# Packing edges by node pairs with PSUM operands, and a fill between the row gathers, in a graph layer kernel

## The chip, the core and the metric

The kernel runs on one core of a Trainium2 chip. The metric is the device time of one execution in microseconds, lower is better. A core has five engines with their own instruction queues: TensorE (PE; its weight loads are listed as PEld), VectorE (DVE), ScalarE (ACT), GpSimd (POOL) and SyncE (SP). SBUF is the working memory of 128 partitions, PSUM the memory that TensorE writes its products to. Transfers run on the core's 16 DMA engines.

## What is computed

A graph layer over 6250 nodes with 256 features and 206,250 edges (`src`, `dst`, sorted by `dst`). The layer norm of `x` goes to two branches, whose sum is added to `x`, and a mixture of experts follows. The part that matters here is the graph branch:

```python
x = h @ W                       # 6250 x 64
el, er = x @ Wl.T, x @ Wr.T     # 6250 x 4 heads
e = jnp.exp(jax.nn.leaky_relu(el[src] + er[dst], negative_slope=0.2))
rowsum = jax.ops.segment_sum(e, src, num_segments=N)
w = e / jnp.maximum(rowsum, EPS)[src]
heads = [jax.ops.segment_sum(w[:, hd:hd + 1] * x[dst], src, num_segments=N) for hd in range(H)]
out = jax.nn.elu(jnp.stack(heads, axis=1) + b).reshape(N, 256)
```

The other branch is linear attention with 4 heads and a row norm. The experts are 8 two-layer networks with weights of 256 x 256; each node's two best are combined.

## The kernel before, in words

The nodes are 49 tiles of 128. The edges are put in a grid of 128 partitions x 1612 columns and have to be brought into the order of their source tile. The kernel has three stages.

**Preparation.** For each group of four tiles `project` (L247) loads rows, computes statistics, transposes, and multiplies with one wide weight matrix; it leaves queries, keys and values in SBUF, and 64 features and 4 right-hand scores of each node in the table `table` in device memory (68 numbers a row). Between the groups, three calls of `sort_batch` (L306) each treat 32 columns of edges, 51 batches in all. A batch compares each edge's tile number with 0 to 49 (`ob`, L320), counts with TensorE (L326), forms ranks (L330 to L365), and moves each edge's two half words (`va`, `vb`) to the partition that its rank names with a one-hot matrix (`ohp`, L372) and a product (L377). The result is `grid`: for each tile, batch and partition at most one edge. `context` (L387) computes the attention's inner matrix among the last batches. A placement stage (L472 to L515) then computes for every tile and batch where its edges go.

**Main stage.** Its order is written out by hand at L907 to L936 for 49 tiles. For each tile, `pack` (L782) moves the tile's edges to 35 columns of 128 edges with one-hot products (`ohc` L785, `rc` L791, `ohp` L799, product L804). It gives `dst_x`, the row numbers of `table`, and `loc`, the source node's place within the tile. `gather` (L824) issues 35 indirect transfers from POOL (L830), one per column. Each brings 128 rows. Rows go to buffers of seven columns, of which there are 12. `sources` (L840) makes the one-hot matrix `oh` (L842), transposes it, and picks the left-hand scores. `weights` (L860) adds the two scores and takes the exponential. `sums` (L873) multiplies each gathered row with its four weights (`v`, L879: 7 columns x 256 products) and sums over the edges of each node with TensorE (L887: a 128 x 128 one-hot matrix against 260 columns, 35 times a tile). `pack` and `gather` for a tile are issued two tiles ahead.

**Fill work.** `attention` (L518) and `finish_steps` (L603: `front`, `route`, eight times `expert`) are generators. `some_more` (L894) takes one step of them after each fifth of a tile, so that they run among the edge work, in groups of four tiles. What is left runs after the last tile (L937).

The instructions of each engine are issued in a fixed order that a scheduler at build time makes of this program. POOL's queue in the main stage holds nothing but the gathers.

Of the kernel before, what the change touches and what calls it, by code (L numbers as in the profile page):

```python
# [17 lines left out]
P = 128  # L18
GT = 4
BW = 32  # L20
PB = 16
CPT = 35
CW = 36
EB = 7
# [3 lines left out]
def tile_gps_layer(  # L28
# [40 lines left out]
    NBT = -(-EC // BW)  # L69
    NB = NT + NT % 2  # L70
    BB = 512 // NB
    BB = 8 if BB > 8 else BB
    assert BW % BB == 0 and CPT % EB == 0
    TW = FO + H
    VW = HF + H
    PW = 3 * HID + TW + H
    KW = 2 * HID + 1
    O_TAB = 3 * HID
    O_EL = O_TAB + TW
    assert NPAD > N and PW <= 512 and last > 0  # L80

    groups = [(t0, min(GT, NT - t0)) for t0 in range(0, NT, GT)]

# [9 lines left out]
    nc.vector.tensor_copy(iota_f, iota_i)  # L93
    iota_h = cp.tile([P, P], F16, name="iota_h")
    nc.vector.tensor_copy(iota_h, iota_i)
    iota_b = cp.tile([P, P], BF16, name="iota_b")
    nc.vector.tensor_copy(iota_b, iota_i)
# [11 lines left out]
    elp = cp.tile([P, NT, 3, H], BF16, name="elp")  # L109
# [3 lines left out]
    grid = cp.tile([P, NT, NBT, 2, 2], F16, name="grid")  # L113
# [39 lines left out]
    def load_edges(pool):  # L153
        return load_ids(pool, "src_i", src, NT * P), load_ids(pool, "dst_i", dst, N)
# [19 lines left out]
    tri = sp.tile([P, P], F16, name="tri")  # L174
    nc.vector.tensor_scalar(tri, iota_f, piota, None, op0=OP.is_gt)
    ones16 = sp.tile([P, P], F16, name="ones16")
    nc.vector.memset(ones16, 1.0)
    delta = sp.tile([NB, NB], F16, name="delta")
    nc.vector.tensor_scalar(delta, iota_f[:NB, :NB], piota[:NB], None, op0=OP.is_equal)
    ntot = cp.tile([NT, NBT], F32, name="ntot")  # L180
# [5 lines left out]
    with tc.tile_pool(name="ids", bufs=1) as lp:  # L186
        src_i, dst_i = load_edges(lp)
        t_i = lp.tile([P, EC], I32, name="t_i")
        t_i2 = lp.tile([P, EC], I32, name="t_i2")

        def twice(a):
            return a[:, :, None].to_broadcast([P, EC, 2])

        nc.vector.tensor_single_scalar(t_i, src_i, 7, op=OP.logical_shift_right)
        nc.vector.tensor_copy(bid, twice(t_i))
        nc.vector.tensor_single_scalar(t_i2, dst_i, 3, op=OP.logical_shift_right)
        nc.gpsimd.tensor_copy(va, twice(t_i2))
        nc.vector.tensor_scalar(
            dst_i, dst_i, 7, 8, op0=OP.bitwise_and, op1=OP.logical_shift_left
        )  # L200
        nc.vector.tensor_single_scalar(src_i, src_i, P - 1, op=OP.bitwise_and)
        nc.vector.scalar_tensor_tensor(t_i, src_i, 1.0, dst_i, op0=OP.add, op1=OP.add)
        nc.gpsimd.tensor_copy(vb, twice(t_i))
# [4 lines left out]
        out=wcat[:, :, O_TAB:O_TAB + FO], in_=gnn_W.rearrange("(c p) f -> p c f", p=P)  # L208
# [21 lines left out]
    for c in range(DC):  # L230
        wt_ps = mps.tile([FO, P], F32, name="tp")
        nc.tensor.transpose(wt_ps, wcat[:, c, O_TAB:O_TAB + FO], ident)
# [4 lines left out]
        nc.scalar.copy(wcat[:, c, O_TAB + FO:PW], wlr_ps)  # L237
# [9 lines left out]
    def project(t0, n):  # L247
# [16 lines left out]
        tab = qw.tile([P, GT, TW], F32, name="tab")  # L264
        for j in range(n):
            t = t0 + j
            xn = qw.tile([P, D], F32, name="xn")
            nc.vector.tensor_scalar(
                xn, xt[:, j, :], stats[:, t, 0:1], rstd[:, t:t + 1],
                op0=OP.subtract, op1=OP.mult,  # L270
# [15 lines left out]
            nc.scalar.copy(tab[:, j, :], pr[:, O_TAB:O_EL])  # L286
            nc.vector.tensor_copy(el[:, t, :], pr[:, O_EL:PW])
            rows = P if t < NT - 1 else last
            k_t = kv[:rows, t, :HID]
            if t == 0:  # L290
                nc.vector.tensor_copy(kmax, k_t)
            else:
                nc.vector.tensor_max(kmax[:rows], kmax[:rows], k_t)
        nc.sync.dma_start(
            out=table[t0 * P:(t0 + n) * P, :].rearrange("(t p) f -> p t f", p=P),
            in_=tab[:, :n, :],
# [9 lines left out]
    def sort_batch(t):  # L306
        c0 = t * BW
        w = min(BW, EC - c0)
        cs = slice(c0, c0 + w)

# [13 lines left out]
        n_ps = sps.tile([NB, BW], F32, name="n_ps")  # L324
        for c in range(w):
            nc.tensor.matmul(  # L326
                n_ps[:, c:c + 1], lhsT=ob[:, c, :], rhs=ones16[:, 0:1], start=True, stop=True
            )
        inc = sw.tile([NB, BW], F32, name="inc")
        nc.vector.tensor_tensor_scan(  # L330
            inc[:, :w], ones[:NB, 0:1].to_broadcast([NB, w]), n_ps[:, :w], 0.0,
            op0=OP.mult, op1=OP.add,
        )
        before = sw.tile([NB, BW, 2], F16, name="before")
        nc.vector.tensor_tensor(
            before[:, :w], inc[:, :w, None].to_broadcast([NB, w, 2]),
            n_ps[:, :w, None].to_broadcast([NB, w, 2]), op=OP.subtract,
        )
        nc.scalar.copy(ntot[:, t:t + 1], inc[:NT, w - 1:w])
        ahead = sw.tile([NB, BW, NB], F16, name="ahead", bufs=1)  # L340
        nc.vector.tensor_tensor(
            pairs(ahead[:, :w]), two(before[:, :w], NB // 2), row(delta, NB // 2), op=OP.mult
# [3 lines left out]
        for i, a in enumerate(range(0, w, BB)):  # L346
            z = min(w, a + BB)
            part = r_ps[:, i, :(z - a) * NB]
            nc.tensor.matmul(part, lhsT=tri, rhs=flat(ob[:, a:z]), start=True, stop=False)
# [4 lines left out]
        nc.scalar.copy(  # L354
            r16[:, :nf * BB, :].rearrange("p (i c) b -> p i (c b)", c=BB),
            r_ps[:, :nf, :BB * NB],
        )
# [3 lines left out]
        rank = sw.tile([P, BW], F16, name="rank")  # L361
        with nc.allow_low_precision("one summand of each sum is not zero"):
            nc.vector.tensor_reduce(rank[:, :w], r16[:, :w], axis=AX.X, op=OP.add)
        rank2 = sw.tile([P, BW, 2], F16, name="rank2")
        nc.vector.tensor_copy(rank2[:, :w], rank[:, :w, None].to_broadcast([P, w, 2]))  # L365
# [9 lines left out]
        g_ps = sps.tile([P, 2 * NB], F32, name="g_ps")  # L375
        for c in range(w):
            nc.tensor.matmul(  # L377
                g_ps, lhsT=ohp[:, c, :], rhs=flat(rv[:, c]), start=(c == 0), stop=(c == w - 1)
            )
        for i in range(2):  # L380
            nc.scalar.copy(
                grid[:, :, t, i, :],
                g_ps[:, i * NB:i * NB + NT, None].to_broadcast([P, NT, 2]),
            )


    def context():  # L387
        km_ps = mps.tile([HID, P], F32, name="tp")
# [23 lines left out]
        for t0, n in groups:  # L412
            kk = kv[:, t0:t0 + n, :HID]
            nc.vector.tensor_sub(kk, kk, krow[:, None, :].to_broadcast([P, n, HID]))
# [26 lines left out]
    batches = list(range(NBT))  # L441
# [6 lines left out]

    rest = kp.tile([P, NT, H], F32, name="rest")
# [4 lines left out]
    nc.vector.tensor_copy(elp[:, :, 2, :], rest)  # L454

# [6 lines left out]
    sw_ctx.close()  # L462
    sx.close()
    kx.close()
    mps_ctx.close()


    gx = ExitStack()
    tp = gx.enter_context(tc.tile_pool(name="placed", bufs=1))
    to_p = tp.tile([P, NT, NBT, 2], F16, name="to_p")  # L470
    to_c = tp.tile([P, NT, NBT, 2], F16, name="to_c")
    with tc.tile_pool(name="place", bufs=1) as pp, tc.tile_pool(  # L472
        name="placep", bufs=2, space=PSUM
    ) as pps:
        inc = pp.tile([NT, NBT], F32, name="inct")
        nc.vector.tensor_tensor_scan(
            inc, ones[:NT, 0:1].to_broadcast([NT, NBT]), ntot, 0.0, op0=OP.mult, op1=OP.add
        )
        over = pp.tile([NT, 2], F32, name="over")
        nc.vector.tensor_reduce(over[:, 0:1], ntot, axis=AX.X, op=OP.max)  # L480
        nc.vector.tensor_scalar(over[:, 0:1], over[:, 0:1], float(P), None, op0=OP.is_gt)
        nc.vector.tensor_scalar(
            over[:, 1:2], inc[:, NBT - 1:NBT], float(CPT * P), over[:, 0:1],
            op0=OP.is_gt, op1=OP.add,
        )
        f_ps = pps.tile([1, 1], F32, name="f_ps")
        nc.tensor.matmul(f_ps, lhsT=over[:, 1:2], rhs=ones[:NT, 0:1], start=True, stop=True)
        nc.vector.tensor_copy(flag, f_ps)
        nc.vector.tensor_tensor(inc, inc, ntot, op=OP.subtract)
        exp_t = pp.tile([NT, NT, NBT], F32, name="exp_t")  # L490
        nc.vector.tensor_tensor(
            exp_t, ident[:NT, :NT, None].to_broadcast([NT, NT, NBT]),
            inc[:, None, :].to_broadcast([NT, NT, NBT]), op=OP.mult,
        )
        for f0 in range(0, NT * NBT, 512):
            f1 = min(NT * NBT, f0 + 512)
            fs = slice(f0, f1)
            q_ps = pps.tile([P, 512], F32, name="q_ps")
            nc.tensor.matmul(
                q_ps[:, :f1 - f0], lhsT=ones[:NT, :], rhs=flat(exp_t)[:, fs],  # L500
                start=True, stop=True,
            )
            q_i = pp.tile([P, 2, 512], I32, name="q_i", bufs=2)
            qf, qc = q_i[:, 0, :f1 - f0], q_i[:, 1, :f1 - f0]
            nc.vector.tensor_scalar(qf, q_ps[:, :f1 - f0], piota, None, op0=OP.add)
            nc.vector.tensor_single_scalar(qc, qf, 7, op=OP.logical_shift_right)
            nc.scalar.copy(
                to_c.rearrange("p b t two -> p (b t) two")[:, fs],
                qc[:, :, None].to_broadcast([P, f1 - f0, 2]),
            )  # L510
            nc.vector.tensor_single_scalar(qf, qf, P - 1, op=OP.bitwise_and)
# [91 lines left out]
    def finish_steps(hps, yps, x2, t0, n, rows_left):  # L603
# [145 lines left out]
        for e in range(NX):  # L749
            expert(e)  # L750
            yield
# [303 lines left out]
```

## Time and profile before

| | |
|---|---|
| median of 3 runs | 3349.35 us (3344.46 to 3351.17) |
| the profiled execution, time / span | 3353.65 / 3351.9 us |
| granted TensorE clock, mean | 0.822 |
| busy: PE / DVE / POOL / ACT | 2427.6 / 2075.7 / 2065.6 / 1051.7 us |
| first and last start of a gather (L830) | 642.1 and 3231.8 us |
| gathers: count, busy, mean | 1715, 2058.7 us, 1200 ns |

A row of a group names the line, the engine, the operation, output and inputs, the shapes and the count; after the bar stand busy time, mean duration of one, and the idle time of the engine just before such instructions with what ended most of it. A row of the timeline has start, duration, engine, line, operation, and in brackets the idle time before it. "issue" is idle time in which the engine waited for nothing that the profile shows. The chain of work that ended last is followed back from the last instruction.

### The profile page before, as it was taken

What the parts mean: (1) busy time and instruction counts of PE and PEld (TensorE: products, weight loads), DVE (VectorE), ACT (ScalarE), POOL (GpSimd) and SP (SyncE); (2) the same over time, 40 slices, a digit from 0 to 9 for tenths busy, and PEclk for the clock granted to TensorE, in tenths of its full rate; (3) what the DMA queues carried; (4) which work ended last, traced back from release to release, by engine and by line L of the source; (5) the groups of instructions that cost most, each with busy time, mean ns of one, the idle gap of its engine ahead of it and who ended that gap; (6) DMA issues with size and microseconds to landing.
All of it is one profiled execution on the core that took longest, in us unless ns stands there. A gap on an engine that the chain in (4) does not pass through costs nothing.

```text
span 3351.9 us, 42641 instructions
## 1 busy us (share of the span) xinstructions
PE 2427.6 (72%) x16398; PEld 1735.7 (52%) x16398; DVE 2075.7 (62%) x3763; ACT 1051.7 (31%) x1888; POOL 2065.6 (62%) x1726
## 2 busy tenths in 40 slices
PE   5878877536464689996866858668686685866858
PEld 3444445325353557675554645546455464554645
DVE  8888899737475656766465564655645556465543
ACT  3322322313243323433233332333323333233322
POOL 0000000278787877788787787877878788787740
PEclk9777777567677799997987979879798797887979
DMA  2000010022222311111111111111111111111110
GB/s 59 23 19 17 18 11 1 7 44 52 50 60 43 94 31 30 35 30 29 25 30 32 30 29 25 30 31 30 30 25 30 31 30 29 25 30 31 31 16 9
DMA packets 106661, 103.22 MB, mean 31 GB/s; under 512 B 42694, under 2 KB 78756, under 8 KB 106452
## 3 DMA queue, kind: packets, MB, share of 16 engines
q0 software_dynamic: 54880, 59.82, 10.4%
q1 hardware_dynamic: 49876, 39.73, 4.0%
q8 instruction: 131, 2.15, 0.3%
q10 hardware_dynamic: 1696, 0.89, 0.1%
q14 instruction: 78, 0.64, 0.1%
HBM read 85.69 MB, written 14.63 MB: 30 GB/s over the span
## 4 chain that ended last, share of the span: by engine, by line
POOL 53%; issue 15%; PE 7%; DMA 4%; DVE 2%; ACT 1%; POOLq 0%; DVEq 0%; ACTq 0%
POOL xe L830 53%; DMA xe<-table,dst_x 4%; PE y_ps L726 2%; PE a_ps L887 2%; PE h_ps L714 2%; DVE v L879 1%; PE y_ps L704 0%; DVE rc L791 0%; DVE ohp L799 0%; PE t_ps L850 0%; PE s_ps L804 0%; ACT ohT L852 0%; ACT hT L722 0%; PE y_ps L653 0%; PE e_ps L854 0%
## 5 line engine op out<-in xcount | busy, mean ns | idle before, releaser
L830 POOL DMA_INDIRECT xe<-table,dst_x x1715 | 2058.7, 1200 | 1152.7 <-DVE loc L819 630.7
L887 PE MATMUL a_ps<-v,oh 128*128 128x260 f32 x3430 | 887.8, 408 | 55.3 <-DVE v L879 51.1
L887 PEld LDWEIGHTS a_ps<-v,oh 128*128 128x128 f32 x3430 | 680.3, 204 | 176.7 <-issue 62.1
L879 DVE TENSOR_TENSOR v<-xe,ew 128x1792 f32<-128x1792 f32 x245 | 493.0, 2019 | 94.7 <-PE a_ps L887 84.9
L726 PE MATMUL y_ps<-w2s,hT 128*128 128x256 f32 x1568 | 396.3, 397 | 115.5 <-DVE x L705 106.8
L875 ACT CAST oh<-oh 128x896 f32<-128x896 bf16 x245 | 230.0, 939 | 783.9 <-PE a_ps L887 770.3
L867 DVE TENSOR_TENSOR z<-z,xe 128x28 f32<-128x28 f32 x245 | 44.5, 188 | 644.1 <-DMA xe<-table,dst_x 611.8
L726 PEld LDWEIGHTS y_ps<-w2s,hT 128*128 128x128 f32 x1568 | 295.6, 196 | 216.9 <-DVE x L705 110.0
L714 PE MATMUL h_ps<-tokT,w1s 128*128 128x512 f32 (+1 forms) x832 | 386.9, 587 | 1.5 <-ACT hT L722 1.4
L804 PE MATMUL s_ps<-rc,ohp 128*128 128x72 f16 x2499 | 117.9, 207 | 352.5 <-DVE ohp L799 253.2
L730 DVE SCALAR_TENSOR_TENSOR x<-y_ps,comb,x 128x256 f32<-128x256 f32 x392 | 183.9, 481 | 256.8 <-PE y_ps L726 255.4
L804 PEld LDWEIGHTS <-ohp 128*128 128x128 f16 x2499 | 104.6, 105 | 370.5 <-DVE ohp L799 346.0
L852 ACT COPY ohT<-t_ps 128x896 bf16<-128x896 bf16 x245 | 220.5, 900 | 136.8 <-PE t_ps L850 129.3
L799 DVE TENSOR_TENSOR ohp<-to_p,iota_h 128x2048 f16<-128x2048 f16 x196 | 193.1, 999 | 7.4 <-PE s_ps L804 7.3
L722 ACT ACTIVATE hT<-h_ps,b1s 128x512 f32<-128x512 f32 (+1 forms) x208 | 135.3, 662 | 188.3 <-PE h_ps L714 179.3
L714 PEld LDWEIGHTS h_ps<-tokT,w1s 128*128 128x128 f32 x832 | 143.1, 192 | 94.9 <-issue 90.5
L842 DVE TENSOR_TENSOR oh<-iota_b,loc 128x896 bf16<-128x896 bf16 x245 | 147.7, 616 | 41.1 <-ACT oh L875 41.1
L870 ACT ACTIVATE ew<-z 128x140 f32<-128x140 f32 x49 | 15.6, 318 | 491.3 <-DVE z L868 491.2
L377 PE MATMUL g_ps<-rv,ohp 128*128 128x100 f16 x1612 | 106.2, 238 | 81.8 <-DVE ohp L372 81.5
L850 PE MATMUL t_ps<-identb,oh 128*128 128x128 bf16 x1715 | 156.3, 234 | 7.1 <-DVE oh L842 6.3
L854 PE MATMUL e_ps<-elp,ohT 128*128 128x12 bf16 x1715 | 81.5, 170 | 102.9 <-ACT ohT L852 100.0
L377 PEld LDWEIGHTS <-ohp 128*128 128x128 f16 x1612 | 98.5, 115 | 103.9 <-DVE ohp L372 96.4
(229 smaller groups left out, 2761.0 us busy)
## 6 DMA issues: line engine op xcount, KB each, us to landing
xe<-table,dst_x POOLq DMA_INDIRECT x1715, 2.4
xt<-in_x_dram SPq DMA_DIRECT2D x24, 512.0 KB
base_y<-xt SPq DMA_DIRECT2D x12, 512.0 KB
yt<-base_y SPq DMA_DIRECT2D x12, 512.0 KB
out_dram<-x SPq DMA_DIRECT2D x12, 512.0 KB
w1s<-in_L_ffn_w_dram SPq DMA_DIRECT2D x8, 256.0 KB
w2s<-in_L_ffn_w_dram SPq DMA_DIRECT2D x8, 256.0 KB
table<-tab SPq DMA_DIRECT2D x12, 136.0 KB
```

Source lines behind the costliest of these rows:

```text
L377: nc.tensor.matmul(g_ps, lhsT=ohp[:, c, :], rhs=flat(rv[:, c]), start=(c == 0), stop=(c == w - 1))
L714: nc.tensor.matmul(h_ps[:, :w], lhsT=w1s[:, e, c, f * P:(f + 1) * P], rhs=tokT[:, c, :w], start=(c == 0), stop=(c == DC - 1),)
L726: nc.tensor.matmul(y_ps, lhsT=hT[:, f, j * P:(j + 1) * P], rhs=w2s[:, e, f, :], start=(f == 0), stop=(f == FC - 1),)
L730: nc.vector.scalar_tensor_tensor(x2[:, j, :], y_ps, comb[:, j, e:e + 1], x2[:, j, :], op0=OP.mult, op1=OP.add,)
L799: nc.vector.tensor_tensor(pairs(ohp[:, :m]), twos(to_p[:, b, t0:t0 + m], P // 2), iota_2.to_broadcast([P, m, P // 2, 2]), op=OP.is_equal,)
L804: nc.tensor.matmul(flat(s_ps), lhsT=ohp[:, t - t0, :], rhs=flat(rc[:, t]), start=(t == 0), stop=(t == NBT - 1),)
L830: nc.gpsimd.indirect_dma_start(out=xe[:, j, :], out_offset=None, in_=table, in_offset=bass.IndirectOffsetOnAxis(ap=dst_x[:, c:c + 1], axis=0),
L850: nc.tensor.transpose(t_ps[:, j, :], oh[:, j, :], identb)
L852: nc.scalar.copy(ohT, t_ps)
L875: nc.scalar.copy(oh32, oh)
L879: nc.vector.tensor_tensor(v[:, :, :HF].rearrange("p j (h f) -> p j h f", h=H), xe[:, :, None, :FO].to_broadcast([P, EB, H, FO]), e_k[:, :, ...
L887: nc.tensor.matmul(a_ps, lhsT=oh32[:, j, :], rhs=v[:, j, :], start=(c == 0), stop=(c == CPT - 1),)
```

## The change

- **Pairs.** Edges are sorted by pairs of tiles: 25 numbers in place of 49 (`NB` is 26, was 50). The grid is kept per 16 columns of edges (101 blocks) in place of 32 (51). `sort_batch` still takes 32 columns. Small steps in it move to ScalarE, and `before` and half of the long reduction are replaced.
- `project` moves the normalised rows to ScalarE and the small copy `el` to POOL; the running maximum of the keys becomes one reduction in `context`. The subtraction of that maximum moves to POOL.
- The placement stage is gone; `pack` now serves a pair of tiles, counts the edges of each **quarter** of a tile (32 nodes) itself, and packs to 2 x 36 columns.
- **Quarters.** A tile's columns are divided among its four quarters; 45 (column, quarter) cells are summed. The weight is put on the one-hot matrix (`ohw`, 4 heads x 32 nodes) and not on the gathered row; the product is `xe` (65 columns as weights, the last one constant 1) against 128 columns. Each tile's result is transposed back with four products (L1060).
- **PSUM operands.** Constants and small operands (`iota_p`, `iota_q`, `edges`, `ew_s`) are copied to one PSUM bank, from which the large VectorE operations take their second operand.
- **Row buffers** are one per tile, three in all. A table row has 69 numbers.
- **Blocks** of tiles for the experts are 4 (nine times), 3, 2, 2, 2, 1, 1, 1, 1 (`sizes`); `hidden` and `result` are interleaved by one expert.
- **Fill.** POOL writes zeros to 480 elements per partition of `pause` ahead of each gather; `behind` fixes the order, so that no gather is next to another.

```diff
+PAUSE = 480
-    NB = NT + NT % 2
+    NQ = -(-NT // U)
+    NB = NQ + NQ % 2
+    sizes = []
+    while sum(sizes) < NT:
+        sizes.append(min(GT, -(-(NT - sum(sizes)) // (GT + 1))))
+    blocks = [(sum(sizes[:i]), n) for i, n in enumerate(sizes)]
...
+    ew_s = bank[:, :CPT * H].rearrange("p (c h) -> p c h", h=H)
+    iota_p = bank[:, words:words + P // 2]
+    iota_q = bank[:, words + P // 2:words + (P + SN) // 2]
+    edges = bank[:, words:words + 2 * NBT]
...
+            ohc = gw.tile([P, PB, U * CW], F16, name="ohc")
+            nc.vector.tensor_tensor(
+                pairs(ohc[:, :m]), twos(to[:, 0, t0:t0 + m], U * CW // 2),
+                iota_2[:, :, :U * CW // 2].to_broadcast([P, m, U * CW // 2, 2]),
+                op=OP.is_equal,
+            )
...
     def gather(dst_x):
-        xes = []
-        for k in range(CPT // EB):
-            xe = gw.tile([P, EB, TW], F32, name="xe", bufs=12)
-            for j in range(EB):
-                c = k * EB + j
-                nc.gpsimd.indirect_dma_start(
-                    out=xe[:, j, :],
+        xe = gw.tile([P, CPT, TW], F32, name="xe", bufs=3)
+        for c in range(CPT):
+            behind(nc.gpsimd.memset(pause[:, c % 2], 0.0))
+            behind(nc.gpsimd.indirect_dma_start(
+                out=xe[:, c, :],
...
+    def sums(i, oh, xe, a_ps):
+        g0, g1 = CELLS[i]
+        n = g1 - g0
+        c0 = i * CS - 1 + g0
+        ohw = gw.tile([P, GC, H, SN], F32, name="ohw")
         nc.vector.tensor_tensor(
-            v[:, :, :HF].rearrange("p j (h f) -> p j h f", h=H),
-            xe[:, :, None, :FO].to_broadcast([P, EB, H, FO]),
-            e_k[:, :, :, None].to_broadcast([P, EB, H, FO]),
+            ohw[:, :n],
+            oh[:, g0:g1, i, None, :].to_broadcast([P, n, H, SN]),
+            ew_s[:, c0:c0 + n, :, None].to_broadcast([P, n, H, SN]),
             op=OP.mult,
         )
-        for j in range(EB):
+        for c in range(c0, c0 + n):
             nc.tensor.matmul(
-                a_ps, lhsT=oh32[:, j, :], rhs=v[:, j, :],
+                a_ps[:, i].rearrange("f h n -> f (h n)"),
+                lhsT=xe[:, c, H:],
+                rhs=ohw[:, c - c0].rearrange("p h n -> p (h n)"),
...
-    for t0, n in groups:
+    for t0, n in blocks:
...
-                if k == 1 and b + 2 < NT:
-                    dst_x, loc = pack(b + 2)
-                    ready[b + 2] = (gather(dst_x), loc)
-                some_more()
-            heads(x2[:, j, :], a_ps)
+                if k == 1 and b % U == U - 1 and b + U + 1 < NT:
+                    pack(b // U + 2)
+                some_more(None if n == GT else (n - j) * S - k)
```

## The prediction

> **What bounds the kernel now.** I read the chain of waits first, then the costliest groups, then the tile `xe`. The chain puts 53% on the gathers and 15% on "issue":
>
> ```profile
> POOL 53%; issue 15%; PE 7%; DMA 4%; DVE 2%; ACT 1%; POOLq 0%; DVEq 0%; ACTq 0%
> ...
> L830 POOL DMA_INDIRECT xe<-table,dst_x x1715 | 2058.7, 1200 | 1152.7 <-DVE loc L819 630.7
> L879 DVE TENSOR_TENSOR v<-xe,ew 128x1792 f32<-128x1792 f32 x245 | 493.0, 2019 | 94.7 <-PE a_ps L887 84.9
> ```
>
> A gather takes 1200 ns in the mean. The tile view of `xe` gives minimum 940 and median 947 ns, and 527 us of idle with "issue" as its end. The timeline of POOL shows what that is: gathers come one after the other with 0.30 us between. Where VectorE is quiet, the period is 1.25 us:
>
> ```profile
> 1551.27 0.95 POOL L830 DMA_INDIRECT xe<-table,dst_x  x1 [0.30 <-DMA xe<-table,dst_x]
> 1552.52 0.95 POOL L830 DMA_INDIRECT xe<-table,dst_x  x1 [0.30 <-issue]
> 1553.77 0.94 POOL L830 DMA_INDIRECT xe<-table,dst_x  x1 [0.30 <-issue]
> ```
>
> Under a large VectorE operation it is longer:
>
> ```profile
> 1512.67 3.95 DVE L879 TENSOR_TENSOR v<-xe,ew 128x1792 f32<-128x1792 f32 x2
> 1512.67 2.83 POOL L830 DMA_INDIRECT xe<-table,dst_x  x1 [0.30 <-issue]
> ...
> 1515.81 1.63 POOL L830 DMA_INDIRECT xe<-table,dst_x  x1 [0.30 <-issue]
> ```
>
> So the span is: 642 us until the first gather, 1715 x 1.511 = 2591 us of gathers almost without a hole, and 119 us after the last, 3352 in all. The profiled time is 1.75 us more, and the median of the runs 4.3 us less than that. POOL waited for finished indices or buffers only about 25 us. TensorE and VectorE have slack in the main stage: in the windows from 1500 to 3000 they are busy 73% and 56%.
>
> **PSUM operands, what they remove.** I set each gather row beside the VectorE row that overlaps it longest. The excess over 945 ns, 438 us in all, lies under L879 (286 us), L799 (58), L842 (27), L785 (17), L791 (12), and 39 under others. All five named have two SBUF inputs. In the changed kernel their successors have one input in PSUM. I take those 400 us as gone and leave 39 us, 0.02 us a gather. If the second input weren't the reason, nothing goes.
>
> **The fill, what it adds.** 1715 writes of 480 elements on POOL, each between two gathers. The queue holds nothing else, so each counts fully unless it lies inside the 0.30 us. The near rows are the first memsets:
>
> ```profile
> 0.24 0.10 POOL L1035 MEMSET const-float32-0.0<- 128x1 f32 x1 [0.24 <-issue]
> 0.28 0.10 POOL L1035 MEMSET const-float32-1.0<- 128x1 f32 x1
> 0.30 0.11 POOL L1035 MEMSET const-bfloat16-1.0<- 128x1 bf16 x1
> 0.33 0.12 POOL L1035 MEMSET const-uint8-127<- 128x1 uint8 x1
> ...
> 0.74 0.20 POOL masks.py:197 MEMSET ident<- 128x128 f32 x1 [0.29 <-POOLq L1035]
> ```
>
> 127 elements more cost 0.105 us, 0.83 ns each; 479 make 0.397 us. The fixed part is 0.10 us by duration, but 0.03 by the distance of two starts. The row alone would give 0.497 us. The Trainium skill's "Perfetto Trace Analysis" (GPSIMD Engine Instruction) says that a GpSimd row's span is unreliable and that the distance between starts is the measure: 0.43 us. Between the two lie 1715 x 0.07 = 120 us. I take 0.43, since these rows do start before the last has ended. Bounds from outside: below, the fill hides in the 0.30 us; above, it brings a second 0.30 us. No row has a fill beside a gather. The likely case is in series: after an idle wait (the gather at 1345.27 us) the row begins 0.27 us after the end of `dst_x`, where a cast waiting for VectorE (11.57 us) begins 0.07 after its own. So part of the 0.30 us looks like the gather's own work on POOL.
>
> Period: 1.25 + 0.43 + 0.02 = 1.70 us; 1715 of them, 2915 us. That is 324 us more than before: the fill costs 737, the PSUM operands give back 400, rounding the rest.
>
> **Preparation.** Per batch the VectorE rows are `ob` 0.965, scan 0.207, `before` 0.200, `ahead` 0.964, `r` 0.966, reduction 1.779, `rank` 0.182, `rv` 0.969 + 0.966, `ohp` 2.255: 9.45 us, 51 times 482. With 26 in place of 50 numbers the five products of 1600 elements have 832. The slope of these rows (4096 against 1600) is 0.517 ns, so each falls to 0.568. The reduction splits into a sum of 384 elements (0.34) and a reduction of 448 (0.58). With the scan of 64 (0.24) and `ohp` as it was: 6.25 us, 319 in all, 163 less. Moved away: `xn` 19.4, running maximum 13.4, `el` 7.5, key subtraction 8.3; added: `shift` about 2.4, the new reduction of 6272 elements about 6.5. That makes 40 less. ScalarE takes `xn`, POOL `el` and the subtraction; POOL is idle here (0 us busy in each window from 100 to 642) and ScalarE 31% busy. Uncovered they would cost some 28 us.
>
> VectorE's busy time from 20 to 600 us falls from 518 to 315 us. TensorE had 454 there. It loses half of `r_ps` (84 us) and about 42 of `g_ps`, and keeps 328. Before, VectorE was busy 89% of this stretch. With two engines equally loaded I expect 83%: 380 us, 200 less. 75 to 88% gives 160 to 222 less.
>
> **Pack and placement.** From the last sort to the first gather there were 37 us (605 to 642), 24 of them placement. Now the first pair needs counting (some 20 small rows, about 10 us, and 3 of waits), then 101 blocks: `ohc` 7272, `rc` 14,544, `ohp` 12,928 elements. At 0.517 ns that is 20 us with overhead. Here a rule speaks against the change: the skill's "VectorE: DVE Perf Modes" (The perf-mode tier table) puts tensor_tensor with any PSUM operand at one element per cycle, and another section of that page caps it at two for 16-bit types. L799 shows 0.999 us for 2048 f16 elements, both in SBUF. At one per cycle the blocks take 38 us. Attention steps stand between them in the new order, about 5.5 us, and 1.5 us at the end. So 40 or 58 us, 3 or 21 more than 37; I take 12. First gather: 642 - 200 + 12 = 454, say 455.
>
> In the main stage that rule costs nothing by itself. VectorE's load per tile: the four `ohw` are 5760 elements, 6.6 us (v took 10.1). `oh` takes 0.9 or 1.7, pack 15 or 23 with counting, other work about 10: 33 or 42 us. A tile's gathers take 59.5. TensorE loses about 6 us of sums (45 x 128 columns for 35 x 260) and 3 of transposes and scores per tile, of some 39 busy. `pack` is issued by pairs and may take over a tile's time, but its indices are needed only after two more tiles of gathers, 119 us; three row buffers give a finished tile as long to come free. The SP queue's transfers are as before: table rows grow by one number in 68. Extra transposes and copies of results (L1057, L1060), about 3 us a tile, lie beside the gathers.
>
> **The end.** The graded blocks leave single tiles, but VectorE's order puts the last tile's rows ahead of expert work of the tile two before it: route and experts of tile 46, then front, route and experts of 47 and 48. In the last stretch before, an expert took 7.07 us for four tiles, 1.8 a tile; alone I take 2.2, so 18 for eight. Route took about 7 us (3257.3 to 3264.4), front about 9 for one tile. 25 + 34 + 36 + 2.4 for landing and 3 for the store: 100 us, 19 less.
>
> **The sum.** 455 + 2915 + 100 = 3470 us of span, 3472 with what lies around it, against 3353.65: 3.5% more. Beside the median, 3468; I forecast 3470. The gain of some 200 us at the start, 400 in the locks and 19 at the end is less than the fill. The period at which nothing changes is (3352 - 555) / 1715 = 1.631 us.
>
> **Rivals.**
> - *The fill hides* (faster). If the 0.30 us are the queue's and not the cores' work, the fill runs in them: 0.945 + 0.497 + 0.02 = 1.46 us; 455 + 2504 + 100 = 3060. For it: gathers wait with "issue" and no cause. Against it: the 0.27 us above. It decides once 0.07 us of the fill overlap. 15%, a third of it partial, up to 3330.
> - *The fill brings its own gap.* 1.25 + 0.50 + 0.30 + 0.02 = 2.07: 4105. Against it: memsets start 0.03 apart. 10%; a part of the gap would give 3700 to 3850.
> - *The consumers bind*: pack at one element per cycle, expert steps and three buffers together make a tile 65 us: 455 + 49 x 65 + 100 = 3740. Against it: 42 us of VectorE. 7%.
> - *The PSUM operands don't free POOL*: period 1.93, 3865. Against it: gathers are short under L730 (195 of 207), which has one of its two inputs in PSUM. 5%.
>
> In series has 63%: start 420 to 500, period 1.65 to 1.78, end 85 to 115 give 3335 to 3670 with its few lowest below 3342. About 0.2% is what a measurement of this kernel can tell from no change. Faster: 15 and 4; same 3; slower 78. The range, 3240 to 3770, takes in series whole, consumers, and the partial forms of the first two.
>
> **What would show it.** First gather at 420 to 500 us; gathers at 945 to 970 ns mean; their starts 1.68 to 1.72 us apart; a memset row of some 0.43 to 0.5 us in each gap; 85 to 115 us after the last gather. VectorE's `ohp` in `pack` at 1.1 or 2.2 us tells the mode. Wrong would be starts 1.45 or 2.05 us apart, gathers that wait for buffers or `dst_x`, or a first gather after 540 us.

## The result, and the profile after

The changed kernel takes 3391.1 us (median of 4 runs, 3387.4 to 3394.39), the kernel before 3350.26 us in the same comparison (3344.46 to 3353.63). The ratio is 1.0123, with a 95% interval from 1.0105 to 1.0142: slower by 1.2%, where the forecast had 3.5%. The direction came out as forecast, the size didn't: the fill, charged with 737 us, costs 620 us of the whole time (below), because it doesn't lie wholly in series with the gathers.

The profiled execution took 3387.4 us, its span is 3385.6 us. The three parts of the span, side by side (before and after from the starts of the first and the last gather in the tile view of `xe`):

| us | before | forecast | after | after minus forecast |
|---|---|---|---|---|
| until the first gather | 642.1 | 455 | 452.9 | -2 |
| first to last gather | 2589.7 | 2915 | 2817.0 | -98 |
| from the last gather to the end | 120.1 | 100 | 115.7 | +16 |
| span | 3351.9 | 3470 | 3385.6 | -84 |

This is the page of the changed kernel, the chain that ended last and the groups behind it. The gathers are now L942, the fill is L941, and `ohw` (L1004) stands where `v` was:

```profile
POOL 69%; PE 8%; issue 8%; DVE 3%; ACT 1%; DMA 1%; POOLq 0%; ACTq 0%; DVEq 0%
...
L942 POOL DMA_INDIRECT xe<-table,dst_x x1715 | 1653.2, 964 | 321.2 <-issue 281.4
L941 POOL MEMSET pause<- 128x480 f32 x1715 | 886.5, 517 | 60.4 <-PE g_ps L432 59.5
...
L1004 DVE TENSOR_TENSOR ohw<-oh,bank 128x1280 f32<-128x1280 bf16 x196 | 322.4, 1645 | 38.9 <-PE a_ps L1011 37.1
```

The mean gather fell from 1200 to 964 ns: nearly all of the delay under VectorE is gone. The gathers' idle time that ends with "issue" fell too, from 504 us before to 281 us. In the gap between two gathers stands a write of 517 ns. The timeline of POOL, at an undisturbed place of the main stage, shows how row and gap fit together:

```profile
1926.92 0.95 POOL L942 DMA_INDIRECT xe<-table,dst_x  x1 [0.17 <-issue]
1927.87 0.51 POOL L941 MEMSET pause<- 128x480 f32 x1
1928.55 0.95 POOL L942 DMA_INDIRECT xe<-table,dst_x  x1 [0.17 <-issue]
1929.50 0.51 POOL L941 MEMSET pause<- 128x480 f32 x1
```

The write begins at the moment the gather's row ends (1926.92 + 0.95 = 1927.87), with no idle time ahead of it. After it, POOL waits 0.17 us, not 0.30. Over all steps the median period is 0.951 + 0.512 + 0.166 = 1.629 us, against 0.945 + 0.305 = 1.25 before. So a fill whose row is 0.512 us long adds 0.379 us: 0.139 us of the old gap has vanished beneath it, and the gather's own row is 0.006 us longer.

### The profile page after: what moved, and what is told of

The parts are those of the page before. It is cut to its first block, busy times and chain, and to the rows that moved or that the text cites. A ratio compares the mean times of both kernels' runs of the same rounds, so it can differ in the third digit from the quotient of the medians.

```text
span 3385.6 us, 41725 instructions
## 1 busy us (share of the span) xinstructions
PE 2142.5 (63%) x15539; PEld 1609.6 (48%) x15539; DVE 2002.6 (59%) x4189; ACT 743.3 (22%) x1535; POOL 2583.9 (76%) x3494
## 4 chain that ended last, share of the span: by engine, by line
POOL 69%; PE 8%; issue 8%; DVE 3%; ACT 1%; DMA 1%; POOLq 0%; ACTq 0%; DVEq 0%
POOL xe L942 45%; POOL pause L941 24%; PE h_ps L739 3%; PE y_ps L755 2%; PE a_ps L1011 1%; PE s_ps L899 1%; DMA xe<-table,dst_x 1%; DVE ohp L426 1%; POOL kv L476 0%; ACT hT L747 0%; DVE rc L889 0%; PE y_ps L730 0%; DVE ohp L894 0%; PE g_ps L432 0%; PE y_ps L679 0%
## 5 line engine op out<-in xcount | busy, mean ns | idle before, releaser
L942 POOL DMA_INDIRECT xe<-table,dst_x x1715 | 1653.2, 964 | 321.2 <-issue 281.4
L941 POOL MEMSET pause<- 128x480 f32 x1715 | 886.5, 517 | 60.4 <-PE g_ps L432 59.5
L1011 PE MATMUL a_ps<-ohw,xe 128*65 128x128 f32 x4410 | 570.4, 288 | 51.6 <-DVE ohw L1004 42.2
L1011 PEld LDWEIGHTS a_ps<-ohw,xe 128*65 128x65 f32 x4410 | 534.5, 148 | 87.9 <-DVE ohw L1004 49.4
L899 PE MATMUL s_ps<-rc,ohp 128*128 128x144 f16 x2525 | 260.0, 276 | 440.2 <-DVE ohp L894 440.0
L739 PE MATMUL h_ps<-tokT,w1s 128*128 128x512 f32 (+3 forms) x1088 | 433.4, 517 | 124.1 <-ACT hT L747 121.9
L1004 DVE TENSOR_TENSOR ohw<-oh,bank 128x1280 f32<-128x1280 bf16 x196 | 322.4, 1645 | 38.9 <-PE a_ps L1011 37.1
L747 ACT ACTIVATE hT<-h_ps,b1s 128x512 f32<-128x512 f32 (+3 forms) x272 | 154.6, 568 | 556.6 <-PE h_ps L739 411.4
L889 DVE TENSOR_TENSOR rc<-ohc,bank 128x1152 f16<-128x1152 f16 (+1 forms) x350 | 226.6, 685 | 5.1 <-PE s_ps L899 1.8
L894 DVE TENSOR_TENSOR ohp<-to,bank 128x2048 f16<-128x2048 f16 (+1 forms) x175 | 193.4, 1105 | 0.0
L426 DVE TENSOR_TENSOR ohp<-rank,iota_h 128x4096 f16<-128x4096 f16 (+1 forms) x51 | 115.7, 2269 | 2.7 <-ACT rank L419 2.6
```

Source lines behind the costliest of these rows:

```text
L426: nc.vector.tensor_tensor(pairs(ohp[:, :w]), two(rank2[:, :w], P // 2), row(iota_h, P // 2), op=OP.is_equal)
L739: nc.tensor.matmul(h_ps[:, :w], lhsT=w1s[:, e, c, f * P:(f + 1) * P], rhs=held["tokT"][:, c, :w], start=(c == 0), stop=(c == DC - 1),)
L747: nc.scalar.activation(held[e][:, f, :w], h_ps[:, :w], AF.Gelu, bias=b1s[:, k:k + 1])
L889: nc.vector.tensor_tensor(pairs(rc[:, :m, i, :]), pairs(ohc[:, :m]), twos(edges_q[:, t0:t0 + m, i, :], U * CW // 2), op=OP.mult,)
L894: nc.vector.tensor_tensor(pairs(ohp[:, :m]), twos(to[:, 1, t0:t0 + m], P // 2), iota_2.to_broadcast([P, m, P // 2, 2]), op=OP.is_equal,)
L899: nc.tensor.matmul(flat(s_ps), lhsT=ohp[:, t - t0, :], rhs=flat(rc[:, t - t0]), start=(t == 0), stop=(t == NBT - 1),)
```

## The experiments

In the short diffs, `-` is the changed kernel unless another is named. "Excess" is the sum over all gathers of what each takes above the median gather.

**The fill left out, and the bank's place.** The first four runs cross the two: with and without the fill, with the bank of small operands in PSUM or in SBUF, and the fill alone put into the kernel before. The kernel before took 3349.98 us beside them.

No fill (the values written to `pause` are used nowhere):

```diff
-            behind(nc.gpsimd.memset(pause[:, c % 2], 0.0))
```

> The changed kernel with the fill left out, the gathers one after another. Common to the theories: first gather near 453 us, end near 116 us after the last. Theory A (POOL stays the bound, the fill's whole cost is 0.379 us of a period of 1.629): period 1.25 + 0.015 = 1.265 us, 453 + 2168 + 116 = 2737 us, 650 us less than the changed kernel. Theory B (without the fill the consumers bind: VectorE waited only about 16 us a tile for rows in the changed kernel, where a tile's gathers take 57.5, so a tile needs about 41 against 44.3 of gathers, more in tiles with pack): gathers wait for buffers or indices, the period is 1.35 us or more, 2880 us or more. Theory C (the fill costs nothing, something else sets the time): about 3390.

The operands back in SBUF, the fill kept:

```diff
-    bank = pv.tile([P, 512], F32, name="bank")
+    bank = gw.tile([P, 512], F32, name="bank", bufs=1)
```

> The changed kernel with the bank of second operands in SBUF in place of PSUM, the fill kept. Theory A (two SBUF inputs hold the gather up at its start): VectorE's large operations are busy some 900 us of the 2817 of gathers, at the ratio of before (400 us of excess for 996 us busy) 360 us come back: about 3750 us, gathers at a mean of about 1.17 us. Theory D (the fill separates the gathers so that the waits mostly fall in it): under 3500. Theory E (the PSUM operands didn't matter): 3390.

Both edits together:

> Second operands in SBUF and no fill. Theory A: 2737 plus 360 to 450 us of excess, 3100 to 3190 us, so the PSUM operands are worth as much without the fill as with it. Theory B (consumers bind without the fill): the excess is partly hidden, and this stands less than 250 us above the kernel without the fill.

The kernel before, with nothing but the fill added (480 elements ahead of each gather, order fixed in the same way):

```diff
...
-                nc.gpsimd.indirect_dma_start(
+                behind(nc.gpsimd.memset(pause[:, c % 2], 0.0))
+                behind(nc.gpsimd.indirect_dma_start(
...
```

> The kernel before with only the fill added, 480 elements ahead of each gather. Theory A (the fill adds 0.379 us to every gather; the excess under VectorE stays 0.255): 3350 + 650 = 4000 us. With the excess falling as VectorE's share of a longer stage falls, 3910. Theory D (the waits fall in the fill): under 3800.

Measured:

| kernel | time us | median period us | excess of gathers us |
|---|---|---|---|
| before | 3349.98 | 1.251 | 434.6 |
| before, with the fill | 3934.63 | 1.628 | 368.1 |
| changed, SBUF operands, no fill | 3066.4 | 1.249 | 322.8 |
| changed, SBUF operands, fill | 3656.7 | 1.629 | 293.5 |
| changed, no fill | 2770.91 | 1.249 | 33.0 |
| changed | 3391.1 | 1.629 | 22.3 |

(Periods and excess are those of one profiled execution each. The time of before is the median of seven runs, the last two are medians of four, the three others are single runs.) Three things follow. In three quite different kernels the fill adds 0.377 to 0.380 us to the median step, whatever VectorE does. The whole time grows by somewhat less than 1715 such steps, 650 us, because some delays and waits shrink beside it: +620 us with PSUM operands, +590 with SBUF operands, +585 in the kernel before. PSUM operands are worth 266 us with the fill and 296 us without, and the excess shows it (271 and 290 us); 360 and up to 450 us had been expected. And what is left of the change, with neither, takes 284 us off the kernel before. From there to the changed kernel: 3350 - 284 - 296 + 620 = 3390.

The kernel without a fill is 17% faster than before (ratio 0.8264, interval 0.825 to 0.8278, from 2768.28 to 2771.24 us), and the best of all that ran; further down stand runs on another chip in which it wasn't faster. It is close to balance, as its chain shows:

```profile
PE 33%; POOL 24%; DVE 14%; issue 12%; ACT 3%; DMA 2%; DVEq 0%; ACTq 0%; POOLq 0%
...
L940 POOL DMA_INDIRECT xe<-table,dst_x x1715 | 1652.0, 963 | 638.9 <-issue 606.5
```

POOL still sets its pace in the main stage: holes beyond the usual gap sum to only 16.8 us there, for all of PE's 33% in the chain.

What a wide VectorE operation does to a gather can be read from two timelines. First with the operands in SBUF and the fill kept:

```profile
1965.32 0.52 POOL L941 MEMSET pause<- 128x480 f32 x1
1965.43 1.76 DVE L1004 TENSOR_TENSOR ohw<-oh,bank 128x1536 f32<-128x1536 bf16 x1 [2.18 <-PE a_ps L1011]
...
1966.01 2.01 POOL L942 DMA_INDIRECT xe<-table,dst_x  x1 [0.17 <-issue]
...
1974.94 1.76 DVE L1004 TENSOR_TENSOR ohw<-oh,bank 128x1536 f32<-128x1536 bf16 x1 [1.92 <-PE a_ps L1011]
...
1975.21 2.32 POOL L942 DMA_INDIRECT xe<-table,dst_x  x1 [0.17 <-issue]
```

The first gather starts 1.18 us before `ohw` ends (1967.19) and takes 1.06 us more than 0.95; the second starts 1.49 us before the end and takes 1.37 more. Each waits out the VectorE operation all but 0.12 us. Of all gathers that start at least 0.2 us before the end of an `ohw`, 143 in this run, the median is all but 0.127 us. The fill at 1965.32 runs beneath the same operation for its usual 0.52. Then the changed kernel, where `ohw` has `bank` in PSUM:

```profile
1936.54 1.74 DVE L1004 TENSOR_TENSOR ohw<-oh,bank 128x1536 f32<-128x1536 bf16 x1
...
1936.95 0.95 POOL L942 DMA_INDIRECT xe<-table,dst_x  x1 [0.17 <-issue]
...
1938.20 1.21 DVE L655 SCALAR_TENSOR_TENSOR x<-x,em 128x1024 f32<-128x1024 f32 x1
1938.58 1.67 POOL L942 DMA_INDIRECT xe<-table,dst_x  x1 [0.17 <-issue]
```

The same operation at the same length, and the gather beneath it takes 0.95 us; the 159 gathers that start so in this run are longer than the median by 0.0005 us in the mean, where those 143 were by 1.02. The next one starts beneath L655, whose two inputs are both in SBUF still: 0.83 us before its end, and 0.72 us longer. Operations like that hold a part of the 22 us of excess that are left; the rest is spread over many lines. Why the operand's place has this effect, no run shows; that it does, the crossed runs do.

**The length of the fill.** Is the price a fixed one plus a rate, or does part of the fill lie beneath the gap? Fills of 48 and 240 elements:

```diff
-PAUSE = 480
+PAUSE = 48
```

> The changed kernel with a fill of 48 elements in place of 480. In the changed kernel a fill row of 0.512 us begins at the end of a gather and the next gather 0.166 us after it: 0.678 between two gathers where it was 0.305. Theory F (0.139 us of the 0.305 aren't the cores' work, and the fill runs beneath them; its cost is its row less 0.139, and nothing below that): a fill of 48 has a row of about 0.14, the period stays 1.25 to 1.26, 2755 to 2790 us. Theory G (the fill adds 0.79 ns an element from the first one on, in series): period 1.25 + 0.038 = 1.288, about 65 us more than without a fill, 2835 us. Theory H (the 0.43 us of the forecast, 0.03 fixed and 0.83 ns an element): 1.32, 2890 us.

> A fill of 240 elements. Theory F: row about 0.30 us, 0.30 + 0.166 between gathers, period 1.417, about 3050 us. Theory G: 1.44, about 3090. Theory H: 1.48, about 3160.

And fills shorter than the hidden part should be, with 1 and 16 elements:

> A fill of one element. The medians of the periods were 1.249 us without a fill, 1.269 with 48 elements, 1.428 with 240 and 1.629 with 480. From 48 on that is a line, 1.229 + 0.83 ns an element, 0.020 below the period without a fill at its start. Theory F (a fill runs beneath 0.139 us of the gap and costs its row less that, nothing while the row is shorter): row about 0.11 us, period 1.249, 2771 us, the same as without. Theory K (the line holds down to one element, so that a gather after another POOL instruction starts sooner than one after a gather): period 1.230, 30 us less, 2740 us. Theory H (0.03 us fixed, in series): 1.28, 2825 us.

> A fill of 16 elements. Theory F: row about 0.13 us, period 1.249 to 1.255. Theory K: 1.242. Theory H: 1.29.

Measured (all but the time are medians over the steps):

| elements | row us | row and waits between gathers us | period us | time us |
|---|---|---|---|---|
| none | - | 0.305 | 1.249 | 2770.9 |
| 1 | 0.117 | 0.305 | 1.249 | see below |
| 16 | 0.130 | 0.305 | 1.255 | see below |
| 48 | 0.158 | 0.316 | 1.269 | 2798.5 |
| 240 | 0.312 | 0.478 | 1.428 | 3049.2 |
| 480 | 0.512 | 0.678 | 1.629 | 3391.1 |

A step with 48 elements and one with a single element, from the timelines of POOL:

```profile
1926.73 0.95 POOL L942 DMA_INDIRECT xe<-table,dst_x  x1 [0.16 <-issue]
1927.68 0.16 POOL L941 MEMSET pause<- 128x48 f32 x1
1928.00 0.96 POOL L942 DMA_INDIRECT xe<-table,dst_x  x1 [0.16 <-issue]
```

```profile
1879.56 0.94 POOL L942 DMA_INDIRECT xe<-table,dst_x  x1 [0.19 <-issue]
1880.50 0.12 POOL L941 MEMSET pause<- 128x1 f32 x1
1880.80 0.94 POOL L942 DMA_INDIRECT xe<-table,dst_x  x1 [0.19 <-issue]
```

With 48 elements 0.16 us of wait is left, about as with 480. With one element 0.19 is left: the row of 0.12 is shorter than what can vanish, and row and wait again make 0.305 us, the gap without any fill. So the price of a fill is what its row exceeds 0.139 us by; below that it is nothing but the few nanoseconds by which the gather's own row varies (0.944 us without a fill, 0.944 to 0.950 with 1 or 16 elements). From 48 to 480 elements the period grows by 0.360 us, 0.83 ns an element. The 48-element kernel is 27.6 us above the one without a fill (run beside a kernel before of 3347.3 us); 1715 times 0.020 us is 34. Its row and time came out a little above what had been expected of a hidden fill (0.158 us for 0.14, 2798.5 for 2790 at most).

The whole times of the two shortest fills (4475.15 and 4472.78 us) can't be set beside the others: they were measured on another chip, where the kernel before took 4188.76 us. The single element was run again, and once more beside the kernel without a fill, to mend that:

> The fill of one element per gather once more, timed beside the kernel before, because the whole time of the earlier run of it came beside a run of the kernel before that took 4189 us. F (a fill lies beneath the first 0.139 us of the gap between two gathers and costs only what is longer): the row of 0.117 us costs nothing, median period 1.249, time 2771 us, within 10 of the kernel without a fill. G (any fill brings a fixed price of its own besides its row): at least 0.03 us a step, 2822 us or more. If the long time was the kernel's own and not that chip's: 4475 us again.

> The kernel without a fill (as in the first of these experiments: the waits of POOL between gathers left out of the computation's way, nothing else changed), run beside the one-element fill. If the long times of the one-element fill were the chip's: this and the one-element fill within 10 us of each other, whatever the kernel before takes there (2771 us where that takes 3350). If they were the kernel's own: 2771 here and 4475 there.

> The fill of one element per gather, on the same chip as the kernel without a fill. F (the fill lies beneath the first 0.139 us of the gap, so a row of 0.117 us costs nothing): within 10 us of the kernel without a fill. G (a fixed price of at least 0.03 us a step): 51 us or more above it. If the fill brings a wait of its own on the other engines: above it by hundreds.

Both ran on further chips, and there all was slow again: the kernel before took 4156.8 to 4251.94 us beside the first and 4212.15 to 4283.95 beside the two others. The kernel without a fill took 4422.34 us, against 2770.91 above, so the long time isn't the fill's. There it is slower than the kernel before (ratio 1.0451, interval 1.0407 to 1.0495): its gain of 17% is shown only where the kernel before takes 3350 us. POOL waits for buffers in these runs, and the engines that should empty them stand idle in pieces of up to 48 us with nothing before them that the profile shows ("remote"). From the waits of the run without a fill:

```profile
POOL xe L940 <- PE a_ps L1009: 1594.2, 42, 79.2
ACT ohT L969 <- remote: 858.3, 33, 48.5
```

Where that comes from wasn't found. The single element took 4471.88 us beside it, 50 us more than none (4460.08 to 4483.53 against 4409.12 to 4445.55). That is about the 51 us that a fixed price of 0.03 us a step would make, but the steps don't show such a price: their median is 1.249 us without and 1.252 with the element. The traces show another difference. With the element, 139 of the 1714 gaps hold an extra wait of 0.1 to 5 us, 126 us together; without it no gap does, and in both runs 47 gaps are longer than that. In the undisturbed run with 48 elements only four gaps are longer than usual. So these waits come with whatever slows these runs; whether they make the 50 us, nothing shows. The price within the step is settled; the whole time with one element, where the kernel before takes 3350 us, is not.

**The graded blocks.** The blocks of experts all of four tiles, with the fill and without:

```diff
-    for t0, n in blocks:
+    for t0, n in groups:
```

> The changed kernel, fill kept, with the even blocks of four (and a last one of one) in place of the graded ones. The end of the changed kernel took 116 us after the last gather's start, the one of before 120. Theory I (the graded blocks shorten nothing, because the experts of the last three tiles stand behind the last tile's rows on VectorE either way): 0 to 10 us more, about 3395. Theory J (they hide the experts of the last full block): 30 us more or worse.

> No fill and even blocks of four. Theory I: within 15 us of the kernel without a fill (2771). Theory J: 30 us more. If fewer, larger expert blocks relieve TensorE, which is busier without the fill (76% of the span), it could be up to 20 us less.

Measured: 3423.47 us with the fill, 32 more than the changed kernel, and 2783.95 without, 13 more. The stage after the last gather lasts 140.3 us in place of 115.7 (140.4 in place of 123.8 without the fill), and the first gather comes 7 us later (5 without). Without the fill the main stage gets 9 us of this back, since POOL waits less for buffers. So the graded blocks are worth some 25 us at the end of the changed kernel, although its end is only 4 us shorter than that of the kernel before: with even blocks it would be 20 us longer. Which other part of the change costs that, no run shows.

## Why the forecast was right in sign and wrong in size

- **What bounds the kernel.** Right. POOL has 69% of the chain (53% before), and waited less than 1 us for buffers in the main stage. The consumers don't bind.
- **PSUM operands.** Right as a sum: above the forecast's base of 945 ns, 33 us are left where it left 39 (22 us above the median gather). But its 400 us was the excess under the old operations. The new ones, put back to SBUF, cause 271 to 290; the rest went with the old operations themselves, since the excess is 323 us where before had 435, with SBUF operands and no fill in both.
- **The rule on the mode of VectorE.** The Trainium skill's "VectorE: DVE Perf Modes" (The perf-mode tier table) would have made an operation with a PSUM operand slower. It doesn't. By shape, 2048 elements of `ohp` take 1210 ns with the bank in PSUM and 1221 ns with the bank in SBUF; 1536 of `ohw` take 1744 and 1754. Changed kernel:

```profile
L894 DVE TENSOR_TENSOR ohp<-to,bank 128x2048 f16<-128x2048 f16 x150 | 181.5, 1210 | 0.0
L1004 DVE TENSOR_TENSOR ohw<-oh,bank 128x1536 f32<-128x1536 bf16 x98 | 170.9, 1744 | 25.3 <-PE a_ps L1011 25.2
```

  With the operands in SBUF:

```profile
L894 DVE TENSOR_TENSOR ohp<-to,bank 128x2048 f16<-128x2048 f16 x150 | 183.2, 1221 | 0.7 <-PE s_ps L899 0.6
...
L1004 DVE TENSOR_TENSOR ohw<-oh,bank 128x1536 f32<-128x1536 bf16 x98 | 171.9, 1754 | 71.3 <-PE a_ps L1011 71.1
```

  The 0.999 us that the forecast gave for 2048 elements of L799 was a slip: a mean over two shapes. The trace of before has 147 rows of 2048 elements with a median of 1215 ns, and 49 of 384.

- **The fill: the step that failed.** "Period: 1.25 + 0.43 + 0.02 = 1.70 us", with the fill wholly in series. The fill adds only 0.379 us to a step, and one of a single element adds nothing that can be told from zero (1.249 to 1.252 us in three runs, 1.249 without): a part of the fill lies beneath the gap. The forecast had named the point from which overlap counts (0.07 us), and had read from the row after `dst_x` that only "part of the 0.30 us" looked like the gather's own work. It then charged all of it. Of the 98 us, (0.43 - 0.379) x 1715 = 87 are this step. Of the rest, 9 are the smaller excess: the mean period is 0.0145 us above the median, not 0.02.

  Read by the rows, two errors of opposite sign stand behind the 0.05 us: the fill's row is 0.512 us and not 0.43, and 0.139 us of it is hidden. The row by duration (0.497) was near to the row that came, but charged in series it would have made the forecast worse, by the 120 us that it names; that the lower number came nearer is luck. The distance of two starts, which the Trainium skill's "Perfetto Trace Analysis" (GPSIMD Engine Instruction) recommends, gives the right 0.379 us when taken from one gather to the next in this very pattern, with and without the fill. Taken from a row of tiny writes at the kernel's start it gave 0.43, with no sign of an overlap. Whether the 0.08 us between 0.512 and 0.43 are the fill's own time or a part of its row that holds nothing up, the periods can't tell.

- **Preparation and pack.** Right as a sum (455 against 452.9), with errors that cancel. VectorE's busy time until the last sort fell to 350 us, not 315. About 16 of these 35 us come from overlap: the rows' durations fell by 184 us in sum but the busy time only by 168, so adding up durations had overstated the part that was cut. About 14 come from per-batch rows longer than estimated (above all the five products, 0.589 to 0.622 us for 0.568), and 5 from the new reduction of the keys, 11.05 us for an estimated 6.5. VectorE is busy 89% of 20 to 413 us, as before, not 83%. `pack` for the first pair lies on the path with 40 us (413 to 453), where the forecast took 49. The timeline of POOL shows both ends of it, the first fill and the first gather:

```profile
413.40 0.50 POOL L941 MEMSET pause<- 128x480 f32 x1 [59.46 <-PE g_ps L432]
452.89 1.14 POOL L942 DMA_INDIRECT xe<-table,dst_x  x1 [38.98 <-DVE loc L918]
```

- **The end.** 115.7 us, not 100. The order was as forecast, the sizes were not: tile 46 takes until 34.9 us after the last gather's start (27 forecast), because its statistics were still to be done and the last rows took 3.8 us to be used; tile 47 takes 41.0 (34), with the `ohw` of the last tile between its steps; tile 48 takes 33.5 (36), the store 6.3 (3). A single tile's expert takes 2.40 us and not 2.2, 5 us of the 16:

```profile
3369.62 0.48 DVE L759 SCALAR_TENSOR_TENSOR x<-y_ps,comb,x 128x256 f32<-128x256 f32 x1 [1.92 <-PE y_ps L755]
3372.02 0.48 DVE L759 SCALAR_TENSOR_TENSOR x<-y_ps,comb,x 128x256 f32<-128x256 f32 x1 [1.92 <-PE y_ps L755]
```

- **The rivals.** The fill hides only by 0.139 of 0.512 us, so that rival's 3060 us fails, though the overlap that it rests on is real. A gap of the fill's own doesn't exist: the wait after it is shorter than before, not doubled. The consumers don't bind with the fill, and hardly without: the kernel without a fill runs the main stage with a mean period of 1.278 us. That the PSUM operands don't free POOL is refuted by the crossed runs.
- **The sign.** It was right by a little. The mean period is 1.6435 us, and the forecast had put the point at which nothing changes at 1.631. With the 100 us that it gave the end, the span would have been 18 us longer than before, not 34.

So the expected gain did come: 284 us from all the rest of the change and 296 us from the operands. The fill gave back 620.

## What to carry to other kernels

Where one engine's queue sets the pace, filler work in its gaps is free only up to the part of the gap that isn't the engine's own work. A short operation put in the gap measures that part: what remains of the wait after it is the engine's own. Put the pieces of such a period together from rows of that very pattern (row, gap, row), and don't carry over a distance of starts from another place; and look at groups by shape before a mean is used as the price of one. When a change bundles a cure and a precaution against the same trouble, cross them in four runs: here the kernel without the precaution was 17% faster than before, and the precaution cost more than that gain. And time both sides of a comparison on the same chip: in the slow runs above, the same kernel was 4.5% slower than before.

## What the runs showed of the hardware that was not expected

- Between two indirect gathers on POOL, a write with a row of up to 0.139 us costs next to nothing (period 1.249 to 1.252 us with 1 element and 1.255 with 16, 1.249 without). From 48 to 480 elements each further one costs 0.83 ns.
- VectorE's 16-bit products with one operand in PSUM are as fast as from SBUF (1210 against 1221 ns for 2048 elements), and gathers beneath such operations are hardly delayed (22 against 293 us of excess over 1715 gathers).
- A fill hardly shields a gather: with SBUF operands the excess is 293.5 us with a fill between gathers and 322.8 without, in the kernel before 368.1 and 434.6.
